# Graph attention on one core: the one-hot of segment ends made by a small matrix product on PE and two passes of ACT, in place of a comparison on DVE

## The chip, the cores and the metric

The kernel runs on one core of a Trainium2 chip. The metric is the device time of one execution in microseconds (us). A core has five instruction queues that run beside each other and meet at semaphores: PE (TensorE, matrix products; PEld is its weight load), DVE (VectorE), ACT (ScalarE), POOL (GpSimd) and SP (SyncE, here only an issuer of DMAs). Each queue executes its own instructions in order.

## The reference

There are 12,500 nodes with 128 features and 212,500 edges, sorted by destination node; each node also has an edge to itself. With 8 heads of 16 features:

```python
h = jnp.maximum(_layernorm(x), 0.0)
q = (h @ Wq.T + bq)          # by node, 8 heads x 16
k = (edge_attr @ Wk.T + bk)  # by edge
v = (h @ Wv.T + bv)          # by node
qs, qd = (q[src], q[dst])
in_m, out_m, diag_m = sum(qs * k), sum(qd * k), sum(qs * qd)   # over the 16 of a head
score = (segment_softmax(in_m / 4, dst) + segment_softmax(out_m / 4, dst)
         + segment_softmax(diag_m / 4, dst)) * edge_weight ** lam
hh = segment_sum(score[..., None] * v[dst], dst)
out = x + leaky_relu(hh @ Wo.T + bo, 0.1)
```

Since edges are sorted by destination, a node's edges are one run, a segment. The softmax and the sums over a segment can be had from scans along the edges, and a node's result is the value of the scan at the last edge of its segment, its end.

## The kernel before

The work is in `ordered_path`. Edges are cut into 416 blocks of 512 (`BE`), and the blocks into five stretches (`S = 5`) that are worked on side by side. A group `g` is one block: stretch `s = g % 5` of round `t = g // 5`. There are 84 rounds (`T`) of five groups, 420 in all. Inside a block, edge e sits at partition p and slot j with e = 4p + j (`JN = 4` slots).

For each group: POOL gathers the rows of q that belong to the sources, by four indirect DMAs (`gather`, L652), nine groups ahead (`LOOK`), with a wait that keeps it from running more than that ahead of PE; SP loads the edge features `ea` (L644). PE transposes them (`turn`, L1089), ACT copies the result to `eT` (L1091), PE multiplies with the weights to `k_ps` (`project`, L1097 and L1099). ACT makes a one-hot of the destination in a window of 42 nodes (`one_hots`, L1083 and L1084); PE spreads the destinations' q by it to `qd_ps` (`spread_q`, L1108; there is one such buffer, so PE waits for DVE's L1119 of the group before), and ACT copies it beside the gathered rows (L1110). DVE makes the products and their sums by head (`logits`, L1119, L1120, L1122).

For each round, the logits are turned so that edges run along a row (`turn_logits`), scanned for the maximum (`scan_max`, L1152 and `gap` L1155), exponentiated by ACT (`powers`), and scanned for the sums (`scan_sums`, L1180). The sums are turned back (`turn_sums`, L1200 and L1201), and PE adds those at segment ends into rows of nodes (`to_rows`, L1213): its weights are `sel`, 128 x 4 x 5 x 42, which is 1 at the edge that is the end of the window's node, and 0 elsewhere. SP stores the rows (`put_rows`, L1225), and they are read again, some rounds later, by the node work (`Nodes`, spread over the groups by `nodes_between`), which ends with the output: 20 pairs of units in the rounds, the rest after them. At s = 4 that node work puts `project_v` (PE, then DVE's L1041) or `project_o` (PE, then ACT's L1051, then DVE's L1052) behind what the round does there.

The order of instructions on each engine is that of the program: `pin` chains each instruction to the one before it on its engine. Small PSUM results (`small`) share three buffers in rotation.

`sel` is made at s = 4 for the round before, by `select`: DVE compares `ends`, which holds for each edge its node's place in the window (1 to 42) if it is the end of a segment and 0 if not, with `places`, a row of 1 to 42. `ends` is made in the preparation, by `edges_5`, from `step`: PE transposes it (`turn_edges`, 16 times), and DVE copies it to SBUF (L735, four times).

The preparation (some 135 us until the first products) loads x, normalizes, makes q for all nodes, and writes it to memory as fp32 (`q_table`, for the gathers) and in three bf16 terms (`q3_table`, for the windows). A branch on the value of `lam` (L725) stands early in it. `edges_5` runs in its last part, inside the loop over `terms_q`, beside the first gathers.

Of the kernel before, what the change touches and what calls it, by code (L numbers as in the profile page):

```python
# [7 lines left out]
F32 = mybir.dt.float32  # L8
BF = mybir.dt.bfloat16
# [463 lines left out]
def ordered_path(ctx: ExitStack, tc: tile.TileContext, flag, x, src, dst, edge_attr, edge_weight,  # L473
# [53 lines left out]
    def stored_at(u):  # L527
# [6 lines left out]
    q_table = dram.tile([NP, F], F32, name="q_table")  # L534
    q3_table = dram.tile([3 * NP, F], BF, name="q3_table")
    rel_d = dram.tile([NB, BE], BF, name="rel_d")
    fa_d = dram.tile([NB, 4, BE], BF, name="fa_d")
    sums = [dram.tile([NP, 2 * H3], F32, name=f"sums{i}") for i in range(S)]

# [3 lines left out]
    nc.gpsimd.iota(jp, pattern=[[1, P]], base=0, channel_multiplier=-1)  # L543
    ident = consts.tile([P, P], F32, name="ident")
    nc.vector.tensor_scalar(ident, jp, 0.0, None, op0=ALU.is_equal)
    places = consts.tile([P, W], F32, name="places")
    nc.gpsimd.iota(places, pattern=[[1, W]], base=1, channel_multiplier=0,
                   allow_small_or_imprecise_dtypes=True)

    third = consts.tile([P, 1], F32, name="third")  # L550
    threes = consts.tile([P, W], F32, name="threes")
# [27 lines left out]
    blank = consts.tile([P, 2 * 2 * H3], F32, name="blank")  # L579
    nc.vector.memset(blank, 0.0)  # L580
    src_i = consts.tile([P, NB, JN], I32, name="src_i")
    ends = consts.tile([P, NB, JN], F32, name="ends")
    bases = consts.tile([1, T, S], I32, name="bases")
    tops = consts.tile([1, T, S], I32, name="tops")
    LOOK, QQ, AHEAD, EA = 9, 11, 6, 7
# [90 lines left out]
    with tc.tile_pool(name="prep", bufs=1) as prep, \  # L676
# [49 lines left out]
            nc.gpsimd.tensor_tensor(weight, weight, lam_sb.to_broadcast([RW, RC]), op=ALU.pow)  # L726


        def turn_edges(of, to, which=range(RB)):
            cols = of.rearrange("r (a p j) -> r a j p", a=RB, j=JN)  # L730
            for a in which:
                t_ps = prep_ps.tile([P, JN, RW], F32, name="t_ps")
                for j in range(JN):
                    pin(nc.tensor.transpose(t_ps[:, j, :], cols[:, a, j, :], ident[:RW, :RW]))
                pin(nc.vector.tensor_copy(to[:, a:NB:RB, :], t_ps.rearrange("p j r -> p r j")))  # L735
# [44 lines left out]
        def edges_5(i):  # L780
            step = got["step"]
            last = step[:, 1:]
            if i == 0:
                bad = got["bad"] = prep.tile([RW, 1], F32, name="bad")
                pin(nc.vector.tensor_reduce(bad, step[:, :RC], AX.X, ALU.min))
            elif i == 1:
                pin(nc.vector.scalar_tensor_tensor(last, last, 0.0, rel, op0=ALU.is_gt,
                                                   op1=ALU.mult))
            elif i < 2 + RB:
                turn_edges(last, ends, [i - 2])  # L790

        def turn_w(i, to):
            w_ps = prep_ps.tile([P, F], F32, name="t_ps")
# [166 lines left out]
        nc.vector.tensor_copy(flag, found[:, 6:7])  # L960


    assert GN // 3 >= 2 + RB
    fin = ctx.enter_context(tc.tile_pool(name="fin", bufs=2))

    def unit_in(to, u):
# [105 lines left out]
    with tc.tile_pool(name="work", bufs=2) as work, \  # L1072
# [110 lines left out]
                d["nd"].append(to)  # L1183

        def select(t):
            sel = work.tile([P, JN, S, W], F32, name="sel")
            at, part = block_rows(t)
            here = ends[:, part].rearrange("p (s b) j -> p j s b", b=G)[:, :, :, at]
            pin(nc.vector.tensor_tensor(sel, here[:, :, :, None].to_broadcast([P, JN, S, W]),  # L1189
                                        places[:, None, None, :].to_broadcast([P, JN, S, W]),  # L1190
                                        op=ALU.is_equal))
            st[t]["sel"] = sel

        def turn_sums(t):
            d = st[t]
# [33 lines left out]
        def later(f, t):  # L1229
            if 0 <= t < T:  # L1230
                f(t)
# [64 lines left out]
        for g in range(end + 2 * S):  # L1296
# [13 lines left out]
            if s == 0:  # L1310
                later(turn_logits, t - 1)
                later(turn_sums, t - 2)
            elif s == 1:
                later(scan_max, t - 1)
            elif s == 2:
                later(powers, t - 1)
                later(to_rows, t - 2)
            elif s == 3:
                later(scan_sums, t - 1)
                fetch(t + 2)  # L1320
                fetch_rows(t + 2)
            else:
                later(select, t - 1)
                later(put_rows, t - 2)
            behind[g + 1, 2] = pinned[products]
            nodes_between(t, s)
# [65 lines left out]
```

## Time and profile before

| what | value |
|---|---|
| median of 3 runs | 2300.62 us (2298.96 to 2305.27) |
| the profiled execution's own time | 2308.75 us |
| its span in the profile | 2307.0 us |
| mean granted PE clock | 0.79 of full speed |
| busy: DVE, PE, POOL, ACT | 2148.9, 1816.2, 1666.3, 1515.6 us |
| first and last gather start (L652) | 93.9 and 2236.6 us |
| first and last product start (L1119) | 137.9 and 2245.4 us |
| `sel` (L1189), 84 instructions | 86.4 us, 1028 ns each |

How to read it: a line of the profile names a source line, an engine, an operation, the tile that it writes and those that it reads, the shape, and how often it ran; then the busy time, the mean time of one, and how long the engine stood idle just before such instructions, with the one whose end released it. In a timeline a row is the start, the duration, then the same names, with the idle time before it in brackets. In windows a row gives a stretch, its length, and the busy time and the number of instructions in it, then the granted PE clock, the busy share of the DMA engines, and GB/s. Times are from the start of the span.

### The profile page before, as it was taken

Reading aid. Unit: us, or ns where it says so; the run is one execution under the profiler, and the core shown is the slowest. Engines: PE = TensorE matmul, PEld = TensorE weight load, DVE = VectorE, ACT = ScalarE, POOL = GpSimd, SP = SyncE. Lnnn points to the kernel's source line nnn. Section 1 sums busy time; section 2 is a strip of 40 time slices with the busy share of each in tenths; the row PEclk is TensorE's granted clock in tenths of the full one; section 3 lists DMA queues with packets and bytes.
Section 4 is the critical chain, followed back from the end, with each engine's and each line's share of the span. In section 5 each row is a group of like instructions: output and inputs, shape, how many; then the busy total and the mean of one; then the engine's idle time right before and its main releaser. Section 6 shows DMA issues by size and latency. Waiting matters only on the chain.

```text
span 2307.0 us, 36031 instructions
## 1 busy us (share of the span) xinstructions
PE 1816.2 (79%) x10629; PEld 1395.9 (61%) x10629; DVE 2148.9 (93%) x2263; ACT 1515.6 (66%) x2797; POOL 1666.3 (72%) x1715
## 2 busy tenths in 40 slices
PE   5458888888878778888777887878788878778876
PEld 4446666666666566666566665666566666556654
DVE  6889999998999999999999999999999999999994
ACT  5667676666676666667666666657666667666772
POOL 3677777777777777777777777777777777777760
PEclk8767777776787797888788778878787788788786
DMA  7785455455454545555544555455555545544531
GB/s 198 242 262 146 144 142 151 135 155 139 129 157 138 149 140 142 154 147 140 156 134 146 145 147 158 136 144 142 152 145 142 153 143 142 158 140 141 142 97 41
DMA packets 306681, 341.04 MB, mean 148 GB/s; under 512 B 137667, under 2 KB 225496, under 8 KB 306165
## 3 DMA queue, kind: packets, MB, share of 16 engines
q1 hardware_dynamic: 244042, 222.69, 32.1%
q0 software_dynamic: 54448, 112.96, 19.3%
q10 hardware_dynamic: 7984, 3.00, 0.5%
q8 instruction: 85, 1.39, 0.2%
q14 instruction: 122, 1.00, 0.1%
HBM read 307.79 MB, written 30.64 MB: 147 GB/s over the span
## 4 chain that ended last, share of the span: by engine, by line
DVE 26%; PE 24%; ACT 16%; issue 16%; DMA 13%; POOL 4%; SPq 1%; DVEq 0%; ACTq 0%; POOLq 0%
DMA qq<-q_table,src_i 10%; PE k_ps L1099 8%; DVE prod L1120 6%; DVE prod L1119 6%; POOL qq L652 4%; PE eT_ps L1089 4%; DVE sum L1180 4%; PE qd_ps L1108 4%; ACT eT L1091 3%; ACT l L1142 3%; ACT relb L1083 3%; PE b_ps L1200 3%; ACT oh L1084 3%; DVE sel L1189 2%; ACT qq L1110 2%
## 5 line engine op out<-in xcount | busy, mean ns | idle before, releaser
L652 POOL DMA_INDIRECT qq<-q_table,src_i x1680 | 1631.5, 971 | 522.9 <-issue 320.6
L1122 DVE TENSOR_REDUCE lT<-prod 128x96 f32<-128x1536 f32 x420 | 736.1, 1753 | 14.4
L1099 PE MATMUL k_ps<-wk,eT 128*128 128x128 f32 x3360 | 603.7, 334 | 66.2 <-ACT eT L1091 58.6
L1099 PEld LDWEIGHTS k_ps<-wk,eT 128*128 128x128 f32 x3360 | 510.3, 232 | 217.0 <-ACT eT L1091 146.1
L1110 ACT COPY qq<-qd_ps 128x512 f32<-128x512 f32 x420 | 245.6, 585 | 578.7 <-PE qd_ps L1108 488.1
L1120 DVE TENSOR_TENSOR prod<-qq,k_ps 128x1024 f32<-128x1024 f32 x420 | 509.4, 1213 | 0.0
L1108 PE MATMUL qd_ps<-win,oh 126*128 126x128 bf16 x1680 | 200.2, 254 | 225.7 <-DVE prod L1119 184.5
L1119 DVE TENSOR_TENSOR prod<-qq,qd_ps 128x512 f32<-128x512 f32 x420 | 284.2, 677 | 66.0 <-ACT qq L1110 37.5
L1089 PE MATMUL eT_ps<-ident,ea 128*128 128x128 f32 x1680 | 332.3, 334 | 12.7 <-DVE found L937 12.7
L1108 PEld LDWEIGHTS <-oh 126*128 126x128 bf16 x1680 | 155.3, 115 | 271.1 <-issue 229.9
L1083 ACT ACTIVATE relb<-relb,before 126x512 bf16<-126x512 bf16 x420 | 306.5, 730 | 0.0
L1091 ACT COPY eT<-eT_ps 128x512 f32<-128x512 f32 x420 | 247.5, 589 | 44.4 <-PE eT_ps L1089 42.3
L1084 ACT ACTIVATE oh<-relb 126x512 bf16<-126x512 bf16 x420 | 264.6, 630 | 17.6 <-DVE flag L960 4.2
L1089 PEld LDWEIGHTS eT_ps<-ident,ea 128*128 128x128 f32 x1680 | 234.8, 176 | 13.0 <-DVE found L937 13.0
L1200 PE MATMUL b_ps<-ident,sum 120*128 120x120 f32 x672 | 147.7, 356 | 91.6 <-ACT l L1142 91.6
L1097 PE MATMUL k_ps<-b,ones 3*128 3x512 bf16 x420 | 191.5, 456 | 10.9 <-DVE prod L1120 9.3
L1213 PE MATMUL w_ps<-back,sel 128*126 128x144 f32 x1344 | 190.1, 295 | 0.6 <-ACT back L1201 0.6
L1200 PEld LDWEIGHTS b_ps<-ident,sum 120*128 120x128 f32 x672 | 104.1, 215 | 138.5 <-ACT l L1142 113.1
L1213 PEld LDWEIGHTS w_ps<-back,sel 128*126 128x126 f32 x1344 | 171.9, 191 | 22.3 <-issue 14.2
L1201 ACT COPY back<-b_ps 128x480 f32<-128x480 f32 x168 | 97.6, 582 | 50.1 <-PE b_ps L1200 50.1
L1152 DVE TENSOR_TENSOR_SCAN u<-l,u,far_ps 120x512 f32<-120x512 f32 x83 | 105.5, 1271 | 0.8 <-ACT l L1142 0.8
L1180 DVE TENSOR_TENSOR_SCAN sum<-keep,sum,up 120x512 f32<-120x512 f32 x83 | 105.9, 1276 | 0.0
(182 smaller groups left out, 1719.1 us busy)
## 6 DMA issues: line engine op xcount, KB each, us to landing
ea<-in_edge_attr_dram SPq DMA_DIRECT2D x419, 256.0 KB
relb<-rel_d SPq DMA_DIRECT2D x84, 630.0 KB
qq<-q_table,src_i POOLq DMA_INDIRECT x1680
win<-q_table SPq DMA_DIRECT2D x420, 31.5 KB
q_table<-q SPq DMA_DIRECT2D x24, 384.0 KB
fa<-fa_d SPq DMA_DIRECT2D x420, 4.0 KB
sums<-rows SPq DMA_DIRECT2D x416, 7.9 KB
q_table<-xq SPq DMA_DIRECT2D x24, 256.0 KB
```

The source lines that it names most:

```text
L652: rows = pin(nc.gpsimd.indirect_dma_start(out=qq[:, j, 0, :], out_offset=None, in_=q_table, in_offset=bass.IndirectOffsetOnAxis(ap=src_i[: ...
L1083: pin(nc.scalar.activation(d, d, AF.Abs, bias=before[:K3]))
L1084: pin(nc.scalar.activation(oh, d, AF.Relu, bias=1.0, scale=-1.0))
L1089: pin(nc.tensor.transpose(eT_ps[:, j, :], eas[g][:, j * F:(j + 1) * F], ident))
L1091: pin(nc.scalar.copy(eT, eT_ps))
L1099: pin(nc.tensor.matmul(k_ps[:, j, :], eTs[g][:, j, :], wk, start=False, stop=(j == JN - 1)))
L1108: pin(nc.tensor.matmul(qd_ps[:, j, :], ohs[g][:, j * P:(j + 1) * P], d["win"][:, s, :], start=(j == 0), stop=(j == JN - 1)))
L1119: pin(nc.vector.tensor_mul(prod[:, :, 2, :], qqs[g][:, :, 0, :], qds[g]))
L1120: pin(nc.vector.tensor_mul(prod[:, :, 0:2, :], qqs[g], ks[g][:, :, None, :].to_broadcast([P, JN, 2, F])))
L1122: pin(nc.vector.tensor_reduce(lTs[t][:, :, s, :], prod.rearrange("p j i (h d) -> p j (i h) d", d=DIM), AX.X, ALU.add))
L1200: pin(nc.tensor.transpose(b_ps[:, j, :], d["nd"][i][:, j:BE:JN], ident[:R, :R]))
L1213: pin(nc.tensor.matmul(w_ps[:, i].rearrange("p s c -> p (s c)"), d["sel"][:, j, lo:lo + 3, :].rearrange("p s w -> p (s w)"), d["back"][:, ...
```

## The change

`ends` isn't held in SBUF any more. Places are written to memory as bf16 in the preparation (`ends_d`: for each block 4 slots of 128), by one DVE copy that reorders and one DMA, in place of the transposes and the copies. In each round SP loads 20 rows of 128 (5 stretches x 4 slots) into a small tile `ends_t` below a row of ones, at s = 3 ahead of the loads for the round after next. At s = 4, `show_ends` lets PE multiply this tile of 21 rows with a constant matrix `shows` (row 0 holds the places 1 to 42, the other rows -1 in their own slot and stretch): the result is place minus end, which is 0 where they are equal. Since both are whole numbers, |d| and then relu(1 - |d|) on ACT is the same one-hot. `shows` is made once in the preparation by `show()`, with two iotas on POOL and two DVE instructions.

```diff
+    ends_d = dram.tile([NB, JN, P], BF, name="ends_d")
...
-    places = consts.tile([P, W], F32, name="places")
-    nc.gpsimd.iota(places, pattern=[[1, W]], base=1, channel_multiplier=0,
-                   allow_small_or_imprecise_dtypes=True)
...
-    ends = consts.tile([P, NB, JN], F32, name="ends")
+    K4 = 1 + S * JN
+    shows = consts.tile([K4, JN, S, W], BF, name="shows")
+    ends_t = [consts.tile([K4, P], BF, name=f"ends_t{i}") for i in range(2)]
+    for to in ends_t:
+        nc.vector.memset(to[0:1, :], 1.0)
...
+        def show():
+            of = prep.tile([K4, JN, S, W], F32, name="of_f", tag="of", bufs=2)
+            nc.gpsimd.iota(of, pattern=[[1, JN], [JN, S], [0, W]], base=1, channel_multiplier=-1,
+                           allow_small_or_imprecise_dtypes=True)
+            nc.vector.tensor_scalar(shows, of, 0.0, -1.0, op0=ALU.is_equal, op1=ALU.mult)
+            nc.gpsimd.iota(of[0:1], pattern=[[0, JN], [0, S], [1, W]], base=1, channel_multiplier=0,
+                           allow_small_or_imprecise_dtypes=True)
+            nc.vector.tensor_copy(shows[0:1], of[0:1])
+
+        show()
...
-            elif i < 2 + RB:
-                turn_edges(last, ends, [i - 2])
+            elif i == 2:
+                ends = of_tile().rearrange("r (a e) -> r a e", a=RB)
+                pin(nc.vector.tensor_copy(ends.rearrange("r a (j p) -> r a j p", j=JN),
+                                          last.rearrange("r (a p j) -> r a j p", a=RB, j=JN)))
+                pin(nc.sync.dma_start(ends_d.rearrange("(r a) j p -> r a (j p)", a=RB), ends))
...
         def select(t):
-            sel = work.tile([P, JN, S, W], F32, name="sel")
             at, part = block_rows(t)
-            here = ends[:, part].rearrange("p (s b) j -> p j s b", b=G)[:, :, :, at]
-            pin(nc.vector.tensor_tensor(sel, here[:, :, :, None].to_broadcast([P, JN, S, W]),
-                                        places[:, None, None, :].to_broadcast([P, JN, S, W]),
-                                        op=ALU.is_equal))
-            st[t]["sel"] = sel
+            ends = ends_t[t % 2]
+            pin(nc.sync.dma_start(ends[1:, :], ends_d[part].rearrange("(s b) j p -> s b j p", b=G)
+                                  [:, at, :, :]))
+
+        def show_ends(t):
+
+            sel = st[t]["sel"] = work.tile([P, JN, S, W], F32, name="sel")
+            for i in range(0, JN, 2):
+                d = small([P, 2, S, W], "d_ps")
+                pin(nc.tensor.matmul(d.rearrange("p j s w -> p (j s w)"), ends_t[t % 2],
+                                     shows[:, i:i + 2].rearrange("k j s w -> k (j s w)"),
+                                     start=True, stop=True))
+                pin(nc.scalar.activation(sel[:, i:i + 2], d, AF.Abs))
+            pin(nc.scalar.activation(sel, sel, AF.Relu, bias=1.0, scale=-1.0))
...
             elif s == 3:
+                later(select, t - 1)
                 later(scan_sums, t - 1)
                 fetch(t + 2)
                 fetch_rows(t + 2)
             else:
-                later(select, t - 1)
+                later(show_ends, t - 1)
                 later(put_rows, t - 2)
```

More of the change, by code (lines that the diff above doesn't have):

```diff
@@ L960, in ordered_path @@
         nc.vector.tensor_copy(flag, found[:, 6:7])
-    assert GN // 3 >= 2 + RB
+    assert GN // 3 >= 3
     fin = ctx.enter_context(tc.tile_pool(name="fin", bufs=2))
```

## The prediction

> **What bounds the kernel now.** Names: a round t is five groups of 512 edges, s = 0 to 4; 84 rounds. I read the page's busy shares first, then the gather's line and the products' line in the view by source line, then both in windows, then the timeline of one round.
>
> ```profile
> PE 1816.2 (79%) x10629; PEld 1395.9 (61%) x10629; DVE 2148.9 (93%) x2263; ACT 1515.6 (66%) x2797; POOL 1666.3 (72%) x1715
> L1189 DVE TENSOR_TENSOR sel<-ends,places 128x840 f32<-128x840 f32 x84 | 86.4, 1028 | 0.0
> ```
>
> By this page DVE (93%) is the bound and the removed `sel` is worth 86.4 us. The next views say otherwise.
>
> ```profile
> L652 POOL DMA_INDIRECT qq<-q_table,src_i x1680: 941/947/7290, 93.9 to 2236.6; - x187
> L1119 DVE TENSOR_TENSOR prod<-qq,qd_ps x420: 657/678/689, 137.9 to 2245.4; 128x512 f32<-128x512 f32 x140
> ```
>
> POOL issues 1680 gathers, four a group, from 93.9 to 2236.6; the products L1119 follow. At the start the products run far behind the gathers; at the end the last product starts 8 us after the last gather ends. In windows, products first, then gathers:
>
> ```profile
> 182.00:482.00 300.00, 42.63 (x63) 0.77 0.50 141
> 600.00:2200.00 1600.00, 212.45 (x314) 0.81 0.52 145
> ```
>
> ```profile
> 182.00:482.00 300.00, 228.07 (x236) 0.77 0.50 141
> 600.00:2200.00 1600.00, 1216.24 (x1259) 0.81 0.52 145
> ```
>
> While a backlog exists (182 to 482 us), products come every 300/63 = 4.76 us, 23.8 a round; gathers every 300/236 x 4 = 5.08, 25.4 a round. From 600 us both go at 5.1 (1259/4 = 315 groups against 314): the products wait for the gathers. POOL sets the pace:
>
> ```profile
> 1329.25 0.95 POOL L652 DMA_INDIRECT qq<-q_table,src_i  x1 [0.31 <-DVE sum L1180]
> 1330.50 0.95 POOL L652 DMA_INDIRECT qq<-q_table,src_i  x1 [0.30 <-issue]
> 1331.75 0.94 POOL L652 DMA_INDIRECT qq<-q_table,src_i  x1 [0.30 <-issue]
> 1333.00 1.32 POOL L652 DMA_INDIRECT qq<-q_table,src_i  x1 [0.30 <-issue]
> 1334.62 0.95 POOL L652 DMA_INDIRECT qq<-q_table,src_i  x1 [0.30 <-issue]
> ```
>
> Start to start it is 1.25 us with a constant gap of 0.30, whoever is named as releaser: nothing it could be waiting for ever lasts longer. 20 x 1.252 = 25.04 us a round is the floor. The one long gather (1.32 instead of 0.95) is what the change touches, with DVE beside it:
>
> ```profile
> 1330.81 1.75 DVE L1122 TENSOR_REDUCE lT<-prod 128x96 f32<-128x1536 f32 x1
> 1332.48 1.02 DVE L1189 TENSOR_TENSOR sel<-ends,places 128x840 f32<-128x840 f32 x1
> 1333.71 0.69 DVE L1041 TENSOR_TENSOR h<-node_ps,score 128x512 f32<-128x512 f32 x1 [0.21 <-PE node_ps L1033]
> ```
>
> The long gather began while `sel`, which reads two SBUF tiles, was running. Over the timeline, of the 84 `sel` 55 have a gather beside them that is lengthened by over 0.06 us; summed over the 84, gathers are 26.2 us longer than 1.25 start to start. `gap` (L1155, also two SBUF tiles) costs 6 us in the same way; the reduce L1122 (one SBUF tile, 420 of them) 1 us, all below 0.02 us each.
>
> **The change part by part.**
>
> *Removed from DVE: 84 x 1.028 = 86.4 us.* The rule of occupancy (the Trainium skill, "Perfetto Trace Analysis", section "Identifying the Most-Contended Engine": the engine with the highest busy share is the bound, and for Vector and GpSimd that share is a fair measure) would make the sum 2308.75 - 86 = 2222. The gather rows disagree: POOL shows 72% and never pauses. I take POOL, so DVE's own time is worth nothing directly.
>
> *The collisions: -26.2.* A rule speaks against this gain: the Trainium skill, "SBUF — State Buffer", section "Who interferes with whom", says that a tensor_tensor with two SBUF inputs holds off only GpSimd work that reads SBUF, and infers that descriptor generation needs the write side, so that it isn't stalled. By that, the term is 0. The rows show 55 lengthened gathers beside `sel`; these gathers also read their indices from SBUF. I take 26.2, and keep 0 as an end. The upper end is 33 (the collisions of L1155 and L1053 gone as well, which nothing here removes).
>
> *Start: +2.7.* `show()` stands after the branch on lam. In the chain of waits DVE is on the path there (47.7 to 64.7 us, then ACT to the first gather). DVE gets a tensor_scalar of 840 columns (L766: 512 in 0.42; 0.6 us), then waits for a POOL iota of 840 that waits for it (jp 128 columns 0.23, due 420 in short runs 1.71: 1.2, at worst 3.4), then a copy of 840 in one row (L804: 384 in 0.35; 0.7). With two handovers 2.7 us, ends 1.5 and 5.5. The first iota and two memsets of one row lie in POOL's 33.5 us wait and DVE's 2.5 us wait for x. The removed iota `places` (0.18) ran before any of this.
>
> *Rest of the preparation.* Removed: 16 transposes on PE and four copies L735 (0.58 each) after 100 us. Added: one DVE copy 104x2048 to bf16 (L750, same size: 1.23 us; L787: 2.28) and one SP DMA of 0.43 MB. These lie beside the gathers and ahead of the first products, which are 33 us behind; only the copy's collision with gathers counts: between 0 and 2.3, I take 0.6. The DMA waits in SP's order ahead of later q3_table stores; the same backlog covers it.
>
> *SP, each round: one DMA of 20 x 256 bytes (about 0.4 us to issue, as L635).* It stands ahead of the relb fetch, at which SP idles 676.7 us in total for ACT (SP's waits, L620 <- ACT oh), so SP arrives early. Its own wait, the product two rounds back, is long over. The x5 win, x5 fa and ea loads behind it move by 0.4 of such idle time. Landing is a few us, use a group later: 0. POOL's queue gets nothing in a round.
>
> *PE, each round: two products of 420 columns with 21 rows, and their loads.* L1144 (20x512 bf16) 0.53, L1164 0.46: 0.45 each, with loads (0.13) 0.8 to 1.1. *ACT: two Abs of 420 from PSUM and one Relu of 840.* L1201 (480) 0.58, L1218 (288) 0.39, so 0.52 each; L1165 (512) 0.61, so 0.9: 1.9 us a round, 160 in all. Neither paces on average (PE 40.8 and ACT 33.5 of each 50 us), but they stand at s = 4, after turn(g+2) and one_hots and ahead of the node work of that group:
>
> ```profile
> 1329.69 0.59 PE L1108 MATMUL qd_ps<-win,oh 126*128 126x128 bf16 x4 [1.32 <-DVE prod L1119]
> 1330.07 1.06 PE L1089 MATMUL eT_ps<-ident,ea 128*128 128x128 f32 x4
> 1331.07 0.60 PE L1031 MATMUL node_ps<-b,ones 3*128 3x512 bf16 x1
> 1331.60 2.08 PE L1033 MATMUL node_ps<-wv,hT 128*128 128x128 f32 x8
> 1333.61 0.60 PE L1097 MATMUL k_ps<-b,ones 3*128 3x512 bf16 x1
> ```
>
> Here L1041 already waited 0.21 for PE's node_ps behind `sel`. With 1.1 us more on PE it starts 1.1 later, and DVE idles where `sel` was. The same holds where project_o runs at s = 4: ACT's L1051 comes behind Abs, Abs, Relu and L1052 behind it, about 1.2 later. There are 20 + 20 such rounds (L1041 x20, L1052 x20, from 620 us on). In the other rounds DVE gets 0.5 to 1.03 back (PE waits 0.4 to 1.5 for L1119 before the next qd_ps). So the round without POOL changes by (40 x 1.1 - 24 x 0.5 to 1.03)/64 = +0.3 to +0.5 from 595 us, and by about +0.5 earlier, where PE follows without a pause.
>
> Is that still under POOL's 25.04? From 600 to 2200 us DVE idles 1600 - 1528.9 = 71 us, 1.1 a round; some 42 us of it goes back to gathers (27.1 directly, the rest through ACT's L1110, which waited 74.4 for them), 0.7 a round. So the round without POOL is 25.4 - 0.7 = 24.7 now and 25.0 to 25.2 then, an estimate. That is even with POOL, so the backlog of the start drains more slowly and some is left: 0 to 7 us, I take 3.4. If it falls behind by nine groups POOL waits too, which isn't near.
>
> *Tail: +1.5.* After the last gather PE is on the path (2252 to 2270); two more products 1.1, ACT's three 0.4 of 1.9 ahead of `back`. The late `sel` stands beside waits: 0 gained. Ends 0 and 4.
>
> Sum against the profiled execution's own 2308.75: -26.2 + 2.7 + 0.6 + 3.4 + 1.5 = -18.0, 2290.8. That execution is 8.1 (0.35%) above the median 2300.62; the same difference on the median gives 2282.6.
>
> **The rivals.**
> (a) *The group s = 4 becomes the bound (slower).* If the node rounds lose 2.1 instead of 1.1 (PE's 1.1, then ACT's passes behind it in series) and the others gain nothing, the round is 24.7 + 40 x 2.1/64 = 26.0; 64 x (26.0 - 25.5, the round of the windows from 600 us) = 32, with start and tail 4.2: 2337. For it: L1041 and L1052 wait there already. Against it: ACT idles 488 us before L1110. It decides from about 25.5 a round.
> (b) *The lock isn't what lengthens the gathers, or another collision takes its place.* The term is 0 to -13; with +4.8: 2305 to 2293, no change.
> (c) *DVE was the bound.* 2300.6 - 86.4 + 4.8 = 2219. Against it: the 0.30 gaps.
>
> **How the numbers follow.** Forecast 0.60 (own range 2272 to 2293), (a) 0.20, (b) 0.17, (c) 0.03. A measurement of this kernel can tell about 0.3% (7 us) from no change: below 2293.7 lie the forecast and (c), 0.62; within, (b) and a little, 0.18; above, (a), 0.20. The range 2264 to 2312 takes in 33 us of collisions below and the mild end of (a) above.
>
> **What would show it.** L652 still at 0.30 gaps, nearly all 0.95 long, and 25.05 a round; L1041 and L1052 with more idle before them; first gather near 96.5; DVE near 90%. Wrong: POOL waits of over 0.31 us or a lag of products that grows along the run means (a); long gathers beside L1155 or with nothing beside them means (b).

## The result and the profile after

The changed kernel takes 2294.24 us (median of 17 runs, 2289.81 to 2302.57), the kernel before, run beside it, 2302.04 (17 runs, 2298.96 to 2307.5): the ratio is 0.9968, with a 95% interval of 0.996 to 0.9976. It is faster by 7.8 us, 0.3%. The forecast was 18 us.

In the changed kernel the gather's line is L656 (L652 before), the products' first line L1137 (L1119), the node work L1059 and L1070 (L1041 and L1052), `gap` L1173 (L1155). First the busy time of the engines from its page, then the gathers and the products in the view by source line:

```profile
PE 1828.4 (80%) x10781; PEld 1396.7 (61%) x10781; DVE 2073.1 (90%) x2180; ACT 1651.9 (72%) x3049; POOL 1645.2 (72%) x1716
L656 POOL DMA_INDIRECT qq<-q_table,src_i x1680: 940/944/6808, 94.8 to 2213.8; - x187
L1137 DVE TENSOR_TENSOR prod<-qq,qd_ps x420: 657/678/690, 142.1 to 2233.4; 128x512 f32<-128x512 f32 x140
```

DVE lost 76 us of work, 3.3% of the span, and the time fell by a tenth of that. The gathers end 22.8 us earlier than before (2214.7 against 2237.6); the last product starts only 12.0 earlier: 18.6 us after the last gather's end, and before it was 7.8. The same two lines in windows, products first, then gathers (columns: window, length, busy us and count, granted clock, DMA share, GB/s):

```profile
182.00:482.00 300.00, 42.68 (x63) 0.79 0.51 145
600.00:2200.00 1600.00, 214.38 (x317) 0.81 0.52 147
```

```profile
182.00:482.00 300.00, 227.17 (x239) 0.79 0.51 145
600.00:2200.00 1600.00, 1211.46 (x1275) 0.81 0.52 147
```

From 600 us there are now 1275/4 = 318.75 groups of gathers against 317 of products. Before, the two went at one pace (1259/4 = 314.75 against 314); now the products fall behind by one to two groups. What DVE waits for says where, changed kernel first, then the kernel before (columns: us in total, times, longest):

```profile
DVE h L1070 <- ACT h L1069: 52.8, 20, 4.5
DVE prod L1137 <- ACT qq L1128: 49.2, 58, 5.1
DVE h L1059 <- PE node_ps L1051: 23.1, 17, 1.9
DVE prod L1137 <- DMA qq<-q_table,src_i: 11.6, 13, 3.2
```

```profile
DVE prod L1119 <- ACT qq L1110: 37.5, 49, 3.8
DVE prod L1119 <- DMA qq<-q_table,src_i: 27.1, 22, 3.1
DVE h L1052 <- ACT h L1051: 11.8, 13, 2.9
DVE h L1041 <- PE node_ps L1033: 1.0, 5, 0.2
```

The waits for the node work's `h` and `node_ps` grew, those for gathers shrank. One of the rounds in which project_o runs, from the timeline:

```profile
2054.62 0.88 PE L1214 MATMUL d_ps<-shows,ends_t 21*128 21x420 bf16 x2
...
2055.86 2.08 PE L1051 MATMUL node_ps<-wo,hT 128*128 128x128 f32 x8
2055.97 0.63 ACT L1102 ACTIVATE oh<-relb 126x512 bf16<-126x512 bf16 x1
...
2056.50 0.91 ACT L1217 ACTIVATE sel<-d_ps 128x420 f32<-128x420 f32 x2
...
2057.45 0.90 ACT L1218 ACTIVATE sel<-sel 128x840 f32<-128x840 f32 x1
...
2058.26 0.58 ACT L1069 ACTIVATE h<-node_ps 128x512 f32<-128x512 f32 x1
...
2058.87 0.69 DVE L1070 TENSOR_TENSOR h<-h,node_ps 128x512 f32<-128x512 f32 x1 [2.75 <-ACT h L1069]
```

PE makes the two new products ahead of `node_ps`, ACT makes its three new passes ahead of `h`, and DVE idles for 2.75 us where it compared for 1.03.

The ledger below is read from the traces. "Lengthened" is the sum of the gathers' intervals over 1.252 us, for the first 40 gathers and for the rest (5.5 to 7.2 us of the first 40 is the first gather itself, in every kernel); the lag is from the end of the last gather to the start of the last product, the tail from there to the end. The two rows of mean lags are the same distance, from the end of a group's gathers to the start of its first product, over all groups of those rounds. The last six columns are experiments that follow; the medians are those of each kernel's own runs.

| us | before | changed | changed, 2nd trace | compared once | PE part alone | ACT part alone | moved behind, 2nd | preparation alone | both edits |
|---|---|---|---|---|---|---|---|---|---|
| first gather | 93.9 | 94.8 | 95.3 | 93.7 | 96.5 | 94.9 | 97.1 | 92.6 | 93.0 |
| lengthened, first 40 | 9.3 | 11.2 | 11.5 | 8.6 | 11.3 | 10.2 | 10.8 | 8.6 | 6.1 |
| lengthened, rest | 31.4 | 5.7 | 8.4 | 3.2 | 2.3 | 7.7 | 6.1 | 5.7 | 3.4 |
| last gather's end | 2237.6 | 2214.7 | 2218.2 | 2208.5 | 2213.2 | 2215.8 | 2217.0 | 2209.9 | 2205.6 |
| lag | 7.8 | 18.6 | 15.9 | 8.9 | 7.8 | 10.9 | 10.9 | 16.1 | 10.9 |
| mean lag, rounds 25 to 40 | 5.0 | 5.9 | 5.2 | 5.2 | 5.9 | 5.5 | 5.8 | 7.6 | 5.1 |
| mean lag, rounds 74 to 83 | 4.7 | 14.8 | 10.8 | 5.9 | 6.0 | 7.5 | 6.9 | 11.8 | 5.8 |
| tail | 61.6 | 60.4 | 61.2 | 60.3 | 62.0 | 59.6 | 63.6 | 59.9 | 63.4 |
| span | 2307.0 | 2293.8 | 2295.4 | 2277.7 | 2283.0 | 2286.3 | 2291.6 | 2285.8 | 2279.9 |
| median of runs | 2302.0 | 2294.2 | 2294.6 | 2281.5 | 2285.9 | 2288.3 | 2291.0 | 2285.4 | 2280.3 |

The first two columns give the result's own sum: start +0.9, lengthened gathers -23.8 (of which the 26.0 beside `sel`, all gone; the others grew by 2.2), lag +10.8, tail -1.2: -13.3, and the spans differ by 13.2. The medians differ by 7.8, because the profiled execution of before (2308.75) lies 6.7 above the median of the 17 runs, and above every one of them, and that of the changed kernel (2295.63) 1.4.

The lag isn't what is left of the backlog of the start. That backlog is 32 to 38 us at the first group, and by rounds 25 to 40 it is gone in all nine traces (mean lag 5.0 to 7.6 us). In the changed kernel a new lag is made after that, in rounds with node work. Why only there, while node work runs from round 19 on, is not known.

### The profile page after: what moved, and what is told of

It reads as the page before. It is cut to its first block, busy times and chain, and to the rows that moved or that the text cites. A ratio compares the mean times of both kernels' runs of the same rounds, so it can differ in the third digit from the quotient of the medians.

```text
span 2293.8 us, 36583 instructions
## 1 busy us (share of the span) xinstructions
PE 1828.4 (80%) x10781; PEld 1396.7 (61%) x10781; DVE 2073.1 (90%) x2180; ACT 1651.9 (72%) x3049; POOL 1645.2 (72%) x1716
## 3 DMA queue, kind: packets, MB, share of 16 engines
q14 instruction: 124, 1.02, 0.2%
## 4 chain that ended last, share of the span: by engine, by line
PE 32%; ACT 22%; DVE 17%; issue 12%; DMA 12%; POOL 3%; SPq 0%; DVEq 0%; ACTq 0%; POOLq 0%
PE k_ps L1117 11%; DMA qq<-q_table,src_i 9%; PE eT_ps L1107 5%; DVE prod L1137 4%; ACT eT L1109 4%; PE qd_ps L1126 4%; DVE sum L1198 4%; ACT relb L1101 4%; ACT oh L1102 3%; DVE prod L1138 3%; ACT l L1160 3%; ACT qq L1128 3%; POOL qq L656 3%; PE b_ps L1226 3%; PE k_ps L1115 2%
## 5 line engine op out<-in xcount | busy, mean ns | idle before, releaser
L656 POOL DMA_INDIRECT qq<-q_table,src_i x1680 | 1608.2, 957 | 522.8 <-issue 321.5
L1140 DVE TENSOR_REDUCE lT<-prod 128x96 f32<-128x1536 f32 x420 | 736.2, 1753 | 14.4
L1117 PE MATMUL k_ps<-wk,eT 128*128 128x128 f32 x3360 | 603.9, 335 | 104.9 <-ACT eT L1109 63.7
L1117 PEld LDWEIGHTS k_ps<-wk,eT 128*128 128x128 f32 x3360 | 511.0, 233 | 252.6 <-ACT eT L1109 148.6
L1128 ACT COPY qq<-qd_ps 128x512 f32<-128x512 f32 x420 | 245.0, 583 | 443.6 <-PE qd_ps L1126 385.4
L1137 DVE TENSOR_TENSOR prod<-qq,qd_ps 128x512 f32<-128x512 f32 x420 | 284.2, 677 | 61.6 <-ACT qq L1128 49.2
L1107 PE MATMUL eT_ps<-ident,ea 128*128 128x128 f32 x1680 | 325.0, 328 | 5.6 <-DVE found L955 5.6
L1107 PEld LDWEIGHTS eT_ps<-ident,ea 128*128 128x128 f32 x1680 | 228.9, 172 | 5.9 <-DVE found L955 5.9
L1226 PE MATMUL b_ps<-ident,sum 120*128 120x120 f32 x672 | 138.7, 337 | 117.6 <-ACT l L1160 117.5
```

What stands on the lines that cost most here:

```text
L656: rows = pin(nc.gpsimd.indirect_dma_start(out=qq[:, j, 0, :], out_offset=None, in_=q_table, in_offset=bass.IndirectOffsetOnAxis(ap=src_i[: ...
L1107: pin(nc.tensor.transpose(eT_ps[:, j, :], eas[g][:, j * F:(j + 1) * F], ident))
L1117: pin(nc.tensor.matmul(k_ps[:, j, :], eTs[g][:, j, :], wk, start=False, stop=(j == JN - 1)))
L1128: pin(nc.scalar.copy(qqs[g][:, :, 1, :], qd_ps))
L1137: pin(nc.vector.tensor_mul(prod[:, :, 2, :], qqs[g][:, :, 0, :], qds[g]))
L1140: pin(nc.vector.tensor_reduce(lTs[t][:, :, s, :], prod.rearrange("p j i (h d) -> p j (i h) d", d=DIM), AX.X, ALU.add))
```

## The experiments

**1. The comparison alone: made once, then replaced by other work on DVE.** Both kernels are the kernel before with `sel` compared in round 0 alone and used in all rounds. The second puts a sum over an SBUF tile of the same size into its place.

```diff
+        sel_once = work.tile([P, JN, S, W], F32, name="sel", bufs=1)
-            pin(nc.vector.tensor_tensor(sel, here..., places..., op=ALU.is_equal))
+            if t == 0:
+                pin(nc.vector.tensor_tensor(sel_once, here..., places..., op=ALU.is_equal))
# the second kernel only:
+            else:
+                pin(nc.vector.tensor_reduce(junk, sel_once ..., AX.X, ALU.add))
```

> The kernel before, with the comparison made once (round 0) and that one-hot used in all rounds: 83 of the 84 comparisons on DVE are left out, and nothing takes their place on PE or ACT. Theory (gathers pace, and the comparison lengthens them): the gathers beside it come down by some 25 us, the products follow, no lag grows: 2302 - 20 to 26, about 2278. Rival 1 (DVE's own time is the bound): 83 x 1.03 = 85 us less, about 2217. Rival 2 (the comparison doesn't lengthen gathers): no change, 2302.

> As a1_no_sel, but in rounds 1 to 83 DVE does a sum over the 840 columns of one SBUF tile (about 1.0 us) in the comparison's place: the same DVE time with one SBUF input instead of two; the comparisons are left out and the sums are not used. Theory (two SBUF inputs hold the gathers up, DVE's time is free): within 4 us of a1_no_sel, about 2280, gathers 0.95 long beside the sum. Rival (it is DVE being busy at that place that costs): as the kernel before, 2302.

Measured: 2281.52 us (0.9916 of before, 0.9898 to 0.9934) without it, and 2283.39 (0.9922, 0.9904 to 0.9939) with the sum in its place. From the second kernel, the engines' busy time, the sum's group, and the gathers by source line:

```profile
PE 1791.8 (79%) x10629; PEld 1380.4 (61%) x10629; DVE 2147.0 (94%) x2263; ACT 1513.6 (66%) x2797; POOL 1636.6 (72%) x1715
L1197 DVE TENSOR_REDUCE junk<-sel 128x84 f32<-128x840 f32 x83 | 84.5, 1018 | 0.0
L652 POOL DMA_INDIRECT qq<-q_table,src_i x1680: 940/944/6628, 92.4 to 2205.2; - x187
```

DVE is as busy as before (94% here, 93% before) with an instruction of the same length (1018 against 1028 ns) at the same place, and the kernel is 19 us faster. So the time of `sel` on DVE was free, and what it cost was the hold on the gathers: beside the 83 sums no gather of the rounds is lengthened by over 0.06 us, beside `sel` 55 are, by 26.0 us in total. `sel` reads two SBUF tiles and the sum one; they also differ in the operation and in the columns written (840 and 84). But in experiment 3 a comparison that writes all 840 columns, from one input in PSUM, lengthens no gather either, so it is neither the comparing nor the writing. In medians the removed cost is 21.3 us (before on this chip 2302.83); the one profiled execution of before put it at 26.

**2. The comparison moved behind the node work.** In the changed kernel, `show_ends` goes after the call that issues the group's node work.

```diff
             else:
-                later(show_ends, t - 1)
                 later(put_rows, t - 2)
             behind[g + 1, 2] = pinned[products]
             nodes_between(t, s)
+            if s == 4:
+                later(show_ends, t - 1)
```

> The changed kernel with show_ends (two products on PE, three passes on ACT) after the node work of s = 4 instead of ahead of it. Theory (the changed kernel gives 11 us back because node work waits behind these in 40 rounds, so products fall behind gathers): L1070 waits as little as before (12 us instead of 53), the lag of products at the end falls from 19 to about 8 us, 2294 - 10 = about 2284. Rival (the sheer load of PE and ACT, wherever it stands): 2294, lag still 15 to 20 us.

> The changed kernel with only the comparison moved behind the node work of its group, once more, beside the preparation alone. On another chip of the same pace 2292.1 with a lag of 12.9. If that was right: 2290 to 2293, and the preparation is worth 10 to 12 us once the products follow. If the moved form was measured too slow there: 2284 to 2287, and the preparation is worth 4 to 6 us as its traces show.

Measured: 2292.09 us (0.9955, 0.9939 to 0.9971) and, on another chip, 2290.97 (0.9954, 0.9941 to 0.9968). Against 2294.2 to 2294.6 that is 2 to 4 us, not the 10 of the first expectation. In the two traces DVE's wait for `h` is 24.5 and 28.1 us instead of 52.8, for `node_ps` 8.5 and 9.0 instead of 23.1; the mean lag of rounds 74 to 83 is 5.5 and 6.9, near that of before, and the last product's 12.9 and 10.9 instead of 18.6. The order of the new work at s = 4 is a cause of the lag; in the medians little of that is seen.

**3. ACT's passes replaced by one comparison on DVE that reads PSUM.** If holding the gathers is all that `sel` cost, a comparison with one input in PSUM should leave the gathers alone.

```diff
-                pin(nc.scalar.activation(sel[:, i:i + 2], d, AF.Abs))
-            pin(nc.scalar.activation(sel, sel, AF.Relu, bias=1.0, scale=-1.0))
+                pin(nc.vector.tensor_scalar(sel[:, i:i + 2], d, 0.0, None, op0=ALU.is_equal))
```

> The changed kernel with DVE comparing the product with 0 straight from PSUM (two instructions of 420 columns, about 0.55 us each) instead of ACT's three passes. No two-SBUF-input comparison is left, ACT is as before, DVE has its 1.1 us a round again, PE keeps the products. If ACT's passes ahead of L1069 are what makes products fall behind: lag at the end about 8, gathers short, 2282 to 2286. If PE's products are: 2294 or more, lag above 15. If the round needs DVE's time back: 2300.

Measured: 2315.45 us (1.0054, 1.0037 to 1.0071), 13 us slower than before and outside all three expectations. The group of the comparison, and products and gathers in the windows:

```profile
L1217 DVE TENSOR_SCALAR sel<-d_ps 128x420 f32<-128x420 f32 x168 | 91.3, 585 | 2.0 <-PE d_ps L1214 2.0
```

```profile
600.00:2200.00 1600.00, 211.87 (x313) 0.79 0.53 146
```

```profile
600.00:2200.00 1600.00, 1211.29 (x1276) 0.79 0.53 146
```

The gathers are as fast as in the changed kernel (1276 of them in the window, 1275 there), and none beside the 168 comparisons is lengthened by over 0.06 us. But the products make 313 groups where the gathers make 319, and the lag reaches 38.9 us. DVE's work alone was free in experiment 1 (2283.39), PE's two products alone are nearly free in experiment 4 (2285.88); together they cost 30 us. DVE waits only 2.0 us for the products themselves; how the two come to hold each other up was not settled. From round 19 on the lag grows all along, from 8.3 us to 38.9: the products' round is 25.59 us, the gathers' 25.10. This is the rival (a) of the prediction, made real by another edit.

**4. PE's part alone and ACT's part alone.** In the first, ACT's passes run in round 0 only; in the second, PE's products do, and the Abs reads an SBUF copy.

```diff
# PE's part alone
-                pin(nc.scalar.activation(sel[:, i:i + 2], d, AF.Abs))
-            pin(nc.scalar.activation(sel, sel, AF.Relu, bias=1.0, scale=-1.0))
+                if t == 0:
+                    pin(nc.scalar.activation(sel[:, i:i + 2], d, AF.Abs))
+            if t == 0:
+                pin(nc.scalar.activation(sel, sel, AF.Relu, bias=1.0, scale=-1.0))
# ACT's part alone
+                if t == 0:
                     d = small([P, 2, S, W], "d_ps")
                     pin(nc.tensor.matmul(d ...))
+                    pin(nc.scalar.copy(d_once[:, i:i + 2], d))
-                pin(nc.scalar.activation(sel[:, i:i + 2], d, AF.Abs))
+                pin(nc.scalar.activation(sel[:, i:i + 2], d_once[:, i:i + 2], AF.Abs))
```

> The changed kernel with PE's two products of a round kept and ACT's three passes made for the first round alone (sel of round 0 is used in all rounds, so the sums are of the wrong segments). On a chip where gathers pace: if PE's products ahead of the node products make the lag, it stays at 16 to 20 us at the last product and the time at 2292 to 2296; if ACT's passes make it, 8 to 11 us and 2284 to 2288; if both are needed, 12 to 14 us and 2288 to 2291. Where other kernels take 2900, it is 1.0 to 1.3% below the changed kernel, as on the two chips before.

> The changed kernel with ACT's three passes of a round kept, reading a tile in SBUF filled in the first round, and PE's two products made for the first round alone (so the sums are of the wrong segments). On a chip where gathers pace, the mirror of PE's part alone: 16 to 20 us of lag and 2292 to 2296 if ACT's passes make it, 8 to 11 us and 2284 to 2288 if PE's products make it, 12 to 14 us and 2288 to 2291 if both are needed. Where other kernels take 2900, it is 1.2 to 1.6% above the changed kernel, as on the two chips before.

> The changed kernel, as the mark on the same chip: 2292 to 2296 where gathers pace, about 2900 where they don't.

Measured on one chip: 2285.88 us with PE's part alone (0.9935, 0.9915 to 0.9956), 2288.28 with ACT's part alone (0.9951, 0.9934 to 0.9967), 2294.6 for the changed kernel (0.996, 0.9941 to 0.998). The lags are 7.8, 10.9 and 15.9 us. DVE's waits, first with PE's part alone, then with ACT's:

```profile
DVE h L1070 <- ACT h L1069: 33.4, 20, 4.2
...
DVE h L1059 <- PE node_ps L1051: 21.3, 14, 1.9
```

```profile
DVE h L1070 <- ACT h L1069: 52.9, 20, 3.6
...
DVE h L1059 <- PE node_ps L1051: 8.0, 8, 1.2
```

Each wait follows its engine: `h` stays at the 53 us of the changed kernel with ACT's passes and falls without them, `node_ps` stays at 21.3 with PE's products (23.1 and 16.7 in the changed kernel) and falls without them. The lag needs both: with either taken away it is 7.8 and 10.9 us at the end and 6.0 and 7.5 in rounds 74 to 83, against 4.7 before. A lag that grows only once the products' round is longer than the gathers' would do this; that is argued. The outcome of the run with ACT's part alone is at the edge of what was expected for PE as the sole cause, the other that for ACT as the sole cause; the two together fit neither.

The same is seen in time from the product of s = 4 to the first of the next round (means over rounds 19 to 82; 26 rounds have no node work at s = 4), and in the round while the backlog of the start lasts (rounds 3 to 11, before any node work; called free rounds below):

| us | no node work | project_v | project_o | rounds 3 to 11 |
|---|---|---|---|---|
| before | 4.45 | 5.13 | 6.29 | 23.87 |
| changed | 3.50 | 5.41 | 7.46 | 23.89 |
| changed, second trace | 3.50 | 5.03 | 7.50 | 23.89 |
| PE's part alone | 3.50 | 5.28 | 6.45 | 22.80 |
| ACT's part alone | 3.50 | 4.55 | 7.50 | 23.69 |
| compared once, none of the change's work | 3.50 | 4.52 | 6.20 | 22.89 |
| sum in its place (experiment 1) | 4.43 | 5.05 | 6.29 | 23.96 |

The last column was not foreseen. Without the comparison a free round is 0.98 us shorter; with the change's work on PE and ACT it is not shorter at all, though no node work stands behind it. PE's part alone keeps the gain, ACT's part alone loses most of it. ACT's 1.9 us of passes delay its copies for the groups that follow: in these rounds it takes 9.35 us from the first product to the third before and 9.85 in the changed kernel, although ACT idles 385.4 us over the run for L1128. A wait that lies in between is PE's at `b_ps` for ACT's copy L1160 (L1142 before): 91.6 us over the run before, 106.9 with PE's part alone, 122.5 with ACT's, 117.5 and 122.1 in the changed kernel. A free round that isn't shorter doesn't make the lag by itself either: the kernel with the sum has 23.96 there, and a mean lag of 6.4 us in rounds 74 to 83. Its project_o is not held up (6.29).

**5. The preparation.** In the first kernel show() stands at the head of the program with a tile for each of its two steps, and ACT makes the reordering copy of the ends; the comparison stays where it was. In the second both this and the move of experiment 2 are made.

```diff
+        of = prep.tile([K4, JN, S, W], F32, name="of_f")
+        nc.gpsimd.iota(of, ...)
+        row = prep.tile([1, JN, S, W], F32, name="row_f")
+        nc.gpsimd.iota(row, ...)
+        nc.vector.tensor_scalar(shows, of, 0.0, -1.0, op0=ALU.is_equal, op1=ALU.mult)
+        nc.vector.tensor_copy(shows[0:1], row)
...
-        show()
...
-                pin(nc.vector.tensor_copy(ends..., last...))
+                pin(nc.scalar.copy(ends..., last...))
```

> The changed kernel with only the preparation edited: show() at the head of the program with two tiles, the reordering copy of the ends on ACT; the comparison stays ahead of the node work. From the traces of the changed kernel (first gather 95.3, 93.0 with the edit; 3.9 us of lengthened gathers beside the copy, gone with it): if the prices add up, the gathers end 6 us earlier, the lag stays at 16 to 20 us or grows by a part of what the gathers gain, since the products can't follow: 2288 to 2292. If the preparation was priced too low, and it makes most of the 14 us between the changed kernel (2294.6) and the one with both edits (2280.3): 2281 to 2285. If it is worth nothing alone, because the products are behind anyway: 2293 to 2296.

> The changed kernel with the comparison behind the node work of its group, show() at the head of the program, and the reordering copy of the ends on ACT. On a chip where gathers pace: 2287.5 to 2289.5 if the start and the copy cost what the traces show (2.5 to 4.5 us under the 2292.1 of the kernel that only moves the comparison), 2291 to 2293 if the preparation costs nothing. Least possible: 2281.5, the kernel with none of the change's work.

Measured: 2285.36 us for the preparation alone (0.9929, 0.9908 to 0.995) and 2280.27 for both (0.9905, 0.9883 to 0.9928). The preparation alone was worth 7 to 9 us (by the ratios and by the medians, on different chips), where adding up the traces' prices gave 3 to 7. First the copy in the changed kernel, with two of the gathers beside it; then the copy in the kernel with both edits:

```profile
108.62 2.58 POOL L656 DMA_INDIRECT qq<-q_table,src_i  x1 [0.30 <-issue]
109.11 1.97 DVE L806 CAST of<-step 104x2048 bf16<-104x2048 f32 x1 [1.02 <-DMA q_table<-q]
...
111.51 2.80 POOL L656 DMA_INDIRECT qq<-q_table,src_i  x1 [0.30 <-issue]
```

```profile
107.02 3.79 ACT L804 CAST of<-step 104x2048 bf16<-104x2048 f32 x1 [2.53 <-DMA q_table<-q]
107.49 0.94 POOL L656 DMA_INDIRECT qq<-q_table,src_i  x1 [0.30 <-issue]
108.74 0.94 POOL L656 DMA_INDIRECT qq<-q_table,src_i  x1 [0.30 <-issue]
109.98 0.94 POOL L656 DMA_INDIRECT qq<-q_table,src_i  x1 [0.30 <-issue]
```

On DVE the copy holds a gather until its own end (111.08; the gather ends at 111.20); the next one is held by the two-input products of the preparation behind the copy. On ACT it takes twice as long and holds nothing. Single traces differ by 1 to 2 us here, so all traces at this pace together say more (means, with the lowest and highest):

| preparation | traces | first gather | gathers 2 to 40 lengthened |
|---|---|---|---|
| before | 3 | 93.3 (92.4 to 93.9) | 2.6 (2.3 to 2.9) |
| as changed | 7 | 95.7 (94.8 to 97.1) | 4.9 (4.3 to 5.3) |
| edited | 2 | 92.8 (92.6 to 93.0) | 1.0 (0.5 to 1.4) |

The change's preparation cost 2.4 + 2.3 = 4.7 us, and the edit gave 2.9 + 3.9 = 6.8 back, near what the medians show. The lag stays (mean 11.8 us in rounds 74 to 83 with the preparation alone): the products simply follow gathers that end earlier. The kernel with both edits beats both kernels: 22 us under before, 14 under the changed one, and level with the 2281.5 of experiment 1 (measured on another chip).

DVE's waits in the kernel with both edits (its lines stand two lower than those of the changed kernel: L1068 is L1070 there, L1057 is L1059):

```profile
DVE prod L1135 <- ACT qq L1126: 51.0, 59, 4.4
DVE prod L1135 <- DMA qq<-q_table,src_i: 30.1, 20, 4.0
DVE h L1068 <- ACT h L1067: 26.7, 20, 3.9
...
DVE h L1057 <- PE node_ps L1049: 8.6, 8, 1.1
```

The products wait for the gathers again (30.1 us, 27.1 before), and the mean lag is 5.8 us in rounds 74 to 83: POOL sets the pace to the end.

**6. The same kernels on two other chips.** On two other chips every kernel, before included, takes 2860 to 2950 us. The times and lags expected below for the other pace could not be tested there.

> The changed kernel with ACT's three passes made once (round 0) and that one-hot used in all rounds; PE's two products and SP's load stay in every round, their results unread. Theory (PE's products, about 1 us, and ACT's passes, 1.9 us, each hold up the node work behind them): L1059's waits stay near 20 us, L1070's fall from 53 to about 25, the lag of products at the end is 9 to 13 us, 2287 to 2291. If ACT's passes alone were the cause: lag 8 or less and as c1_late in the waits, 2286. If PE's alone: 2294, lag 18.

> The changed kernel with PE's products made once; ACT's three passes read that product from SBUF in every round (the one-hot is that of round 0). Theory: L1059's waits fall to a few us, L1070's stay at 35 to 50, lag at the end 10 to 15, 2288 to 2292. If PE's products alone were the cause: lag 8, 2286. If ACT's alone: 2294, lag 18.

> c1_late, and in the preparation: show() at the very start (its two iotas into tiles of their own, so that DVE waits for none in the middle), and the reordering copy to ends_d on ACT instead of DVE. Theory (the preparation costs the gathers some 6 us: a start 1 to 1.5 later, and 1.6 to 3.7 beside the DVE copy): c1_late's 2292 - 4 to 6 = about 2287, first gather at 94, no long gathers beside the copy. Rival (the preparation is covered by the 33 us that products are behind): as c1_late, 2292.

> The changed kernel itself, on the chip of this call, for a comparison with the three others: 2294, lag at the end 15 to 20 us, L1070's waits about 50 us, L1059's about 20.

> The changed kernel with the two products of a round kept on PE and ACT's three passes made for the first round alone (sel of round 0 is used in all rounds, so the sums are of the wrong segments). If PE's two products ahead of the node products make the lag of the last products behind the last gathers (18.7 us in the changed kernel, 7.8 before), it stays at 16 to 20 us and the time at 2292 to 2296. If ACT's passes make it, the lag falls to 8 to 11 us and the time to 2284 to 2288. If both are needed, between them: 12 to 14 us of lag and 2288 to 2291.

> The changed kernel with ACT's three passes of a round kept, reading a tile in SBUF that was filled in the first round, and PE's two products made for the first round alone (so the sums are of the wrong segments). The mirror of the run with PE's part alone: if ACT's passes make the lag, it stays at 16 to 20 us and the time at 2292 to 2296; if PE's products make it, 8 to 11 us and 2284 to 2288; if both are needed, 12 to 14 us and 2288 to 2291.

> The changed kernel with three edits: the products and passes of the comparison behind the node work of their group (as in the run where only that was moved: 2292.1, lag 12.9), show() at the head of the program with two tiles, so that nothing of it stands between the branch on lam and the first gathers, and the reordering copy of the ends on ACT instead of DVE. If the start and the copy cost what the traces show (0.5 to 0.9 us at the first two gathers, 1.6 to 3.7 us of lengthened gathers beside the copy), it gains 2.5 to 4.5 us over the moved form: 2287.5 to 2289.5. If the preparation costs nothing, 2291 to 2293. The kernel that makes the comparison once and has none of the change's work took 2281.5, which is the least that it can reach.

> The changed kernel once more, as the mark for the three others on the same chip. If the chip is like that of the first runs: 2292 to 2296, against 2300 to 2304 before.

| ratio to before on the same chip | one chip (before 2916.9) | the other (before 2896.7) |
|---|---|---|
| changed | 0.9945 (0.9926 to 0.9964) | 0.9979 (0.9965 to 0.9992) |
| PE's part alone | 0.9836 (0.9797 to 0.9875) | 0.9871 (0.9852 to 0.9889) |
| ACT's part alone | 1.0106 (1.007 to 1.0143) | 1.0097 (1.0081 to 1.0113) |
| both edits | 1.0059 (1.0042 to 1.0076) | 1.0074 (1.0058 to 1.0089) |

The changed kernel there, products and then gathers in the same window, and two of POOL's waits:

```profile
600.00:2200.00 1600.00, 169.39 (x249) 0.70 0.40 115
```

```profile
600.00:2200.00 1600.00, 950.23 (x998) 0.70 0.40 115
```

```profile
POOL qq L656 <- issue: 479.6, 1342, 3.0
POOL qq L656 <- PE b_ps L1226: 238.4, 72, 6.4
```

POOL pauses for up to 6.4 us before a gather, the products are about 50 us behind the gathers from the first rounds to the last, and a round takes 32 us. A group then takes 6.4 us, and the nine groups at which POOL has to wait for PE are 58 us (an estimate from these figures): gathers don't set the pace there, so these runs say nothing on the lag. Instructions of DVE and ACT are as long as elsewhere (L1140 1753 ns in both, L1128 583 ns), and PE's a little longer (L1117 360 ns against 335), 142 us of busy time in the whole run; the rest of the 586 us are waits between engines, many of which the trace puts down to nothing it knows. What makes them so long was not settled. The order of the kernels is another one there: the kernel with both edits, elsewhere the best, is slower than before.

## Why the prediction was wrong

The direction and the main mechanism were right: POOL's gathers set the pace, the two-input comparison held them, and the 26 us of that are gone from the trace. The time fell by 7.8 us instead of 18. Of the 10.2 us that are missing, 5.3 are in the step from the profiled execution to the median, and the rest is the lag of the products, 10.8 us where 3.4 was put, less what smaller terms gave. By its own steps:

- *DVE's 86.4 us are worth nothing.* Right: experiment 1 puts 84.5 us of another instruction there, for 1.9 us (2283.39 against 2281.52, with intervals that overlap). The rule of occupancy, by which the sum was 2222, doesn't hold here; rival (c) falls.
- *The collisions, -26.2.* Right in the pair of traces (-26.0), and what spoke against it doesn't hold for these gathers: a tensor_tensor with two SBUF inputs does hold an indirect DMA's issue on POOL, and a sum with one doesn't. Whether that is because these gathers read their indices from SBUF was not told apart. In the medians it is -21.3, as experiment 1 measures it; rival (b) falls as the main account.
- *The median follows the profiled execution.* This step failed: "the same difference on the median" took over 5.3 us by which the two profiled executions differ more than the medians. The one of before lies above all 17 runs; which part of its trace is longer than usual stays open.
- *Start, +2.7.* The first gather is 0.9 and 1.4 us later in the two traces of the changed kernel. Over all traces it is 2.4 (the table of experiment 5): right.
- *The copy, +0.6, ends 0 and 2.3.* It cost 1.6 us in one trace and 4.0 in the other (with the products right behind it); over all traces gathers 2 to 40 are 2.3 us longer than before, the upper end. That the preparation could be had for less than before (first gather 92.8 instead of 93.3, 1.0 us of lengthened gathers instead of 2.6) was not seen.
- *The products' backlog, +3.4, ends 0 and 7.* **The term of the sum that failed**, in size and in what it was: it is 10.8 us in the first trace of the changed kernel and 8.1 in the second. The prediction let the backlog of the start drain more slowly, so that some is left. But it drains (mean lag 5.9 and 5.2 us in rounds 25 to 40, 5.0 before), and a new lag is made in the rounds with node work (14.8 and 10.8 us in rounds 74 to 83, 4.7 before). The round without POOL was put at 25.0 to 25.2 and called "even with POOL". From round 43 to 83 the products' round is 25.33 us and the gathers' 25.10 (25.26 and 25.14 in the second trace): 0.1 to 0.2 us too long, over 40 rounds, is 5 to 9 us. What such a difference costs over the run was not worked out in the prediction.
- Of the parts of that round, project_o's was right (+1.2 forecast, +1.2 measured in both traces), as was the gain of 0.5 to 1.03 in rounds without node work (0.95). In project_v's rounds 1.1 was forecast and +0.3 and -0.1 measured. What was left out is ACT: its passes were priced only where node work stands right behind them, with its idle time as cover elsewhere. The rounds 3 to 11 show no cover: 0.98 us gained, and all of it given back in the next groups. How much of the lag comes from this and how much from the node work held up was not told apart.
- *Tail, +1.5.* It is -1.2 and -0.4: nothing.
- Another term was missing: gathers beside `gap` (L1173) are lengthened by 9.5 and 11.1 us (counted over 0.06 us each) against 5.8 before, the mild form of rival (b). With less waiting for gathers the products stand at another phase to them; that this is the cause is only argued. It isn't ACT's part: without it, it is 6.5 with PE's part alone, but 9.6 in experiment 3.
- *Rival (a)* was the right one to fear. It put the limit at a round of 25.5; the changed kernel's is 25.27 over rounds 19 to 83, the kernel of experiment 3 got to 25.59 and lost 13 us.
- *The signs*: gaps of 0.30, nearly all gathers 0.95 long, and DVE near 90% came out. "A lag of products that grows along the run" was named as the sign of rival (a); it came out as well, at a third of that rival's price.

## What to carry to other kernels

When a producer sets the pace with a fixed interval, remove what holds the producer, and then look at the consumers' round: a consumer that is 0.2 us a round slower than the producer loses that in every round, and once it has caught up, faster rounds don't help, since it can't run ahead of the producer. Work moved to an engine with idle time is not covered by that idle time if it stands ahead of an instruction that others wait for; behind the last such instruction of its group it cost 2 to 5 us less here. The inputs of an instruction mattered more than its length: the same 1.02 us on DVE cost 21 us with two SBUF inputs and 1.9, within the noise, with one.

## What the runs showed of the hardware that was not expected

A one-input DVE copy from f32 to bf16 (1.97 us) holds a gather on POOL to its end as the two-input instructions do, while the one-input sum (1753 ns, 420 of them, and 1018 ns, 83 of them) doesn't, nor does the comparison from PSUM (585 ns, 168 of them). The Trainium skill, "SBUF — State Buffer", section "Who interferes with whom", counts casts among what can take the port pair that DVE shares with GpSimd, and reduces on trn2 among what never does; the trace agrees on both. It differs from what that section infers for the two-input case, as told above.

The kernel before took 2302 to 2303 us on three chips and 2897 and 2917 on two others; the changed kernel's trace has DVE and ACT instructions of the same length there, PE's somewhat longer (L1117 360 ns against 335), and a granted clock of 0.71 instead of 0.80. A change that is tuned against the pace of the gathers is tuned for the first kind.
